# A two-layer transformer on one core: the order of the seven products, the spread of the w2 butterflies, and DMA-turned probabilities for two more units of the first attention

## Chip, core and metric

The kernel runs on one core of a Trainium2 chip. Its time is the device time of one execution in microseconds (us); the median of 3 runs of the kernel before is 749.98 us (749.78 to 750.11). The engines are TensorE (PE for matmuls, PEld for its weight loads), VectorE (DVE), ScalarE (ACT), GpSimd (POOL) and SyncE (SP), whose queue issues all DMAs here. An engine works its own queue strictly in order, and waits where an instruction's input, or the buffer that it writes, isn't ready.

## What is computed

Four layers, one after the other, on x of 4 sequences x 256 tokens x 256 features in fp32. Each adds its result to x and begins with a layer norm. Cut to its core, the reference is

```python
# layer 0, attention: 16 query heads, 8 key/value heads, window 128
q, k, v = einsum(x, q_kernel), einsum(x, k_kernel), einsum(x, v_kernel)
q, k = rope(rms_norm(q)), rope(rms_norm(k))
probs = softmax(where(mask, q @ k.T * 0.088, -big))
x = x + einsum(probs @ v, out_kernel)
# layer 0, FFN
h = silu(x @ w_gate) * (x @ w_up)
x = x + keep_two_largest_of_four(h) @ w_down
# layer 1, attention: 16 heads, causal
k, q, v = W_K x, W_Q x, W_V x
x = x + W_O (softmax(mask(k, q) / sqrt(128)) @ v)
# layer 1, FFN
hidden = fwht(silu(x @ W1.T) * (x @ W3.T))     # Walsh-Hadamard transform over 1024
x = x + hidden @ W2.T
```

## The kernel before, in words

**Layout.** A tile has 128 partitions. A sequence has two tiles of 128 tokens. Everything is fp32, and an fp32 matmul is two TensorE passes in the trace (x2 rows), while a transpose of a 128 x 128 tile is one. PSUM, where matmuls write, has eight banks; pool `ps1` (`bank()`) rotates four, and the other four belong by turns to `ps2` (`half()`, `wide()`) and `st_pool` (`st()`).

**Units and stages.** Each attention runs over 16 units of work, one for a sequence and a group of four heads. In the first attention unit n is sequence n // 4, group n % 4; in the second it is sequence n % 4, group n // 4. `pipelined` calls the stages of a unit in successive steps, so that several units are under way at once, and after each step calls what stands in `behind` for it (mostly output projections). In `attention0` the stages are project, rotate, turn, score, split, join and attend, with lags 0, 0, 1, 2, 3, 4, 4, called within a step in the order project, join, split, score, rotate, turn, attend. The calls set each instruction's place in the program; a scheduler then fixes the order within each engine's queue when the program is built, and `issue_after` pins an instruction behind another one of its engine.

**First attention.** `project0` multiplies (rows pj, L437), DVE forms the rope parts qs and qc (L442), `rotate0` adds them (L461), sums squares (ss, L462) and lets POOL make the factors r (L481) and scale k (L484). q is turned from the sixth unit on by a DMA (`qpl`, `qplT`), k by TensorE (tr_k, L510), which ACT copies (kT, L511). `probabilities` makes scores (sc, L204 and L205), masks them with a running maximum on DVE (L207), exponentiates on ACT with row sums (L217) and scales on POOL by the reciprocal (L225). Each unit has two pairs of heads, kk = 0 and 1, each with a tile p of 128 x 768.

**Turning the probabilities.** p @ v needs p with the tokens turned. There are two ways. By DMA: `planes` lets POOL separate p into 16-bit halves (pl, L242), a DMA transposes them (plT, L251), and `joined` puts the halves together again (pT, L262), in the first attention with one ACT copy for each pair. By TensorE: `transposed` makes six transposes of 128 x 128 for each pair (tr_p, L237), and ACT and DVE copy three each (pT, L238). In the first attention the DMA way serves all units but the last three (13, 14 and 15), in the second all but the last two. The tiles pl and plT of the first attention share four buffers. Then come av (L385, L389), its copy zT (L393) and the output projection po (L294).

**The seven products.** The second attention's q, k and v and the last FFN's two hidden products are formed by 2 x 2 blocks with seven block products in place of eight. `left_of` (L615) and `right_of` (L624) make the sums of blocks on DVE; `seven_products` issues the products into three PSUM accumulators x, z and y and combines them through copies u on ACT (L632, L638, L641, L650) and sums on DVE (L635, L644, L647). In `project1` the generators for q and k (banks qk_x, qk_z, qk_y) and for v (bank v_x, and one bank v_zy that holds z in its first half and y in its second) advance in turn. For each product the first flag says whether it begins a new accumulation in its bank.

**Butterflies.** The Walsh-Hadamard transform is folded into w2. `hadamard` does the part within 128 rows on TensorE (ph, L793) with an ACT copy (L796), and three rounds of sums and differences across row groups on POOL (L805), four instructions each. Before, `prepare` and its neighbours call one round behind each of the steps 11 to 14 of the second attention (the first call is the TensorE part).

Of the kernel before, what the change touches and what calls it, by code (L numbers as in the profile page):

```python
# [24 lines left out]
ALU = mybir.AluOpType  # L25
AX = mybir.AxisListType

P = 128
B, T, D = 4, 256, 256
# [19 lines left out]
def two_layers(ctx, tc, consts, tables, x, wq, wkv, wo, w_gate, w_up, w_down,  # L49
               w_k, w_q, w_v, w_o, w1, w3, w2, out):  # L50
    nc = tc.nc
# [92 lines left out]
    last_of = {}  # L144
# [94 lines left out]
        return pT  # L239

    def copy_gpsimd(o, i):
        nc.gpsimd.tensor_scalar(o, i, 1.0, 1.0, ALU.mult, ALU.mult)  # L242

    def planes(p, tile):

# [70 lines left out]
    def attention0():  # L316
        with tc.tile_pool(name="attn0", bufs=2, reuse_waits="tile", side="right") as own:
            xnT, factors = {0: normed(0)}, {}


            cos_s = own.tile([P, NT, 2, HD], F32, name="cos_s", bufs=1)
            sin_s = own.tile([P, NT, 2, HD], F32, name="sin_s", bufs=1)
            with tc.issue_after(last_of["norm"].ins):
                for t in range(NT):
                    for tab, at in ((cos_s, 0), (sin_s, 256)):
                        src = angles[:, at + t * HD : at + (t + 1) * HD]
                        nc.vector.tensor_tensor(
                            tab[:, t], src.unsqueeze(1).to_broadcast([P, 2, HD]), scl, ALU.mult
                        )

            def project(n, _):
                b, g = divmod(n, 4)
                held = project0(own, xnT[b], g, cos_s, sin_s)
                if g == 1 and b + 1 < B:
                    factors[b + 1] = moments(b + 1)
                if g == 2 and b + 1 < B:
                    with tc.issue_after(last_of["qc"].ins):
                        xnT[b + 1] = normed(b + 1, factors[b + 1])
                return held

            def rotate(n, held):
                rot, v = held
                rot, qT_planes, r = rotate0(rot, n >= 6, last_of["mx"] if 2 <= n < 14 else None)
                return rot, qT_planes, v, r

            def turn(n, held):
                rot, qT_planes, v, r = held
                return *turn0(own, rot, qT_planes, half if 6 <= n < 14 else bank), v, r

            def score(n, held):  # L350
                qT, kT, v, r = held
                ps = [
                    probabilities(
                        qT, kT, (2 * kk, 2 * kk + 1), mask0,
                        r[:, :, 2 * kk : 2 * kk + 2].rearrange("p t h -> p h t"),
                    )
                    for kk in range(2)
                ]
                return ps, v

            def split(n, held):
                ps, v = held
                return ps if n >= B * 4 - 3 else [
                    planes(p, own_planes) for p in ps
                ], v

            def own_planes(shape, name):
                return own.tile(shape, U16, tag="pl", name=name, bufs=4)

            def join(n, held):  # L370
                ps, v = held
                return [
                    transposed(ps[kk]) if n >= B * 4 - 3 else joined(ps[kk], ((
                        (nc.scalar.copy, slice(0, 2), last_of["exp"]),
                        (nc.scalar.copy, slice(0, 2), last_of["exp"]),
                    )[kk],)) for kk in range(2)
                ], v

            def attend(n, held):
                pTs, v = held  # L380
                zT = page("zT")
                for kk in range(2):
                    pT = pTs[kk]
                    av = bank([2, T], "av")
                    nc.tensor.matmul(  # L385
                        av, lhsT=v[:, 0, kk, :], rhs=pT[:, :, 0:T], start=True, stop=False,
                        skip_group_check=True,
                    )
                    nc.tensor.matmul(  # L389
                        av[:, :, P:T], lhsT=v[:, 1, kk, :], rhs=pT[:, :, T:],  # L390
                        start=False, stop=True, skip_group_check=True,
                    )
                    nc.scalar.copy(zT[:, 2 * kk : 2 * kk + 2, :], av)  # L393
                return zT

            def out(b, t, gs, kept=False):

                def emit(done):
                    zTs, w = [done[4 * b + g] for g in gs], wo_sb[:, 4 * gs[0] :]
                    if not kept:  # L400
                        project_out(bank([D], "po"), zTs, w, b, t)
                    else:
                        with tc.issue_after(last_of[0].ins):
                            project_out(half([D], "po"), zTs, w, b, t)
                return emit

            behind = {
                4 * b + 6 + 2 * k + t: [out(b, t, (2 * k, 2 * k + 1))]
                for b in range(B) for k in range(2) for t in range(NT)
            }  # L410
            behind = {step: fns for step, fns in behind.items() if step < 16}
            behind[17] = [lambda _: xn_f.append(normed(0))]
            behind[19] = [
                lambda _: xn_f.append(normed(1)), *(out(2, t, (2, 3), True) for t in range(NT)),
                *(out(3, t, (0, 1, 2, 3)) for t in range(NT)),
            ]
            pipelined(
                (project, rotate, turn, score, split, join, attend), (0, 0, 1, 2, 3, 4, 4),
                behind, (0, 5, 4, 3, 1, 2, 6),
            )  # L420
# [203 lines left out]
            nc.vector.tensor_tensor(t[i], a, b, op)  # L624
        return w11, w21, w22, t[3], t[0], t[1], t[2]

    def seven_products(product, x, z, y, c11, c12, c21, c22, shape):


        u = [late.tile(shape, F32, tag="u", name="u", bufs=4) for _ in range(3)]  # L630
        product(x, 1, True)
        nc.scalar.copy(u[0], x)  # L632
        yield
        product(z, 2, True)
        nc.vector.tensor_tensor(c11, z, u[0], ALU.add)  # L635
        yield
        product(y, 5, True)
        nc.scalar.copy(u[1], y)  # L638
        yield
        product(x, 6, False)  # L640
        nc.scalar.copy(u[2], x)  # L641
        yield
        product(y, 3, False)
        nc.vector.tensor_tensor(c12, y, u[2], ALU.add)  # L644
        yield
        product(x, 7, False)
        last_of["sum"] = nc.vector.tensor_tensor(c22, x, u[1], ALU.add)  # L647
        yield
        product(x, 4, False)
        last_of["copy"] = nc.scalar.copy(c21, x)  # L650
        yield
# [23 lines left out]
    def attention1(finish_ffn0):  # L675
# [48 lines left out]
        behind = {n + 3: [out(n)] for n in range(9)}  # L724
        behind[0] = [lambda _: finish_ffn0()]

        def prepare(_):
            w2h.extend(hadamard(w2_raw))
            w2h[1][0](_)

        behind.setdefault(11, []).append(prepare)
        for i in range(1, 4):
            behind.setdefault(11 + i, []).append(lambda _, i=i: w2h[1][i](_))

        def prepare_ffn1(_):
            with tc.issue_after(last_of["sum"].ins):
                r_ffn1.extend(factors_ffn1(half) for half in range(2))

        behind[15] = [out(12)]
        behind[16] = [  # L740
            lambda _: xn_f.append(normed(0)),
            prepare_ffn1,
        ]
# [8 lines left out]
    def project1(x, w):  # L752
# [11 lines left out]
        def product_v(o, i, first):  # L764
# [10 lines left out]
        zy = st([P, 2, 256], "v_zy")  # L775
        products.append(seven_products(
            product_v, bank([256], "v_x"), zy[:, 0], zy[:, 1],
            *(c[:, t, m, :] for t in range(2) for m in range(2)), [P, 256],
        ))
        for _ in zip(*products):  # L780
            pass
# [3 lines left out]
    def hadamard(w2_raw):  # L785


        a, b = (late.tile([P, NF, D], F32, tag=t, name=f"w2_{t}") for t in ("qkw", "qkt"))

        def within(_):  # L790
            for f in range(0, NF, 2):
                ph = bank([2, D], "ph")
                nc.tensor.matmul(  # L793
                    ph, lhsT=had, rhs=w2_raw[:, f : f + 2, :], start=True, stop=True
                )
                nc.scalar.copy(a[:, f : f + 2, :], ph)  # L796

        def across(s, src, dst):
            i = src.rearrange("p (a two s) d -> p a two (s d)", two=2, s=s)
            o = dst.rearrange("p (a two s) d -> p a two (s d)", two=2, s=s)  # L800
            half = s * D // 2
            for k, op in enumerate((ALU.add, ALU.subtract)):
                for n in range(2):
                    cols = slice(n * half, (n + 1) * half)
                    nc.gpsimd.tensor_tensor(  # L805
                        o[:, :, k, cols], i[:, :, 0, cols], i[:, :, 1, cols], op
                    )

        return b, (
            within, lambda _: across(1, a, b), lambda _: across(2, b, a),  # L810
            lambda _: across(4, a, b),
        )

    def factors_ffn1(half):

# [150 lines left out]
```

## Time and profile before

| what | value |
|---|---|
| median of 3 runs | 749.98 us |
| the profiled execution's own time | 749.92 us |
| its span, first to last instruction | 748.1 us |
| PE busy | 737.5 us, 99% of the span |
| ACT / DVE / POOL busy | 401.6 / 465.9 / 331.0 us |
| granted TensorE clock | 1.00 in every slice |
| end of the first attention (last av) | about 264.5 us after the span's start |
| second attention | about 357 to 665 us |
| last FFN | about 665 us to the end |

The execution's own time is 1.8 us more than the span: what lies before the first and behind the last profiled instruction. A row of the timeline reads: start, length, engine, line, operation, output <- inputs, count, and in brackets the idle time of the engine ahead of it with what ended it. Matmuls overlap, so the length of a row of matmuls says less than the distance between starts: in this trace one pass with a moving tile of 128 columns starts 0.111 us after the one before, one with 256 columns 0.216 us, one with 512 columns 0.43 us, wherever nothing is waited for.

### The profile page before, as it was taken

The numbers are of one execution on the slowest core, as the hardware profiler recorded it, in microseconds if no ns is written. First come the engines' busy times: TensorE is split into PE (matmuls) and PEld (weight loads), VectorE is DVE, ScalarE is ACT, GpSimd is POOL, SyncE is SP. The second block draws the span as 40 slices with busy tenths as digits, with TensorE's granted clock in tenths as the row PEclk, the third lists the DMA queues.
The fourth block names the chain that finished last, engine by engine and source line by source line (L and its number), as shares of the span: only waits on it lengthen the run. The fifth ranks groups of instructions, "written<-read, shape, count | busy, mean of one in ns | idle before, by whom it ended". The sixth has DMA issues, their size and how long they took to land.

```text
span 748.1 us, 11666 instructions
## 1 busy us (share of the span) xinstructions
PE 737.5 (99%) x3980; PEld 603.2 (81%) x3980; DVE 465.9 (62%) x1402; ACT 401.6 (54%) x985; POOL 331.0 (44%) x475
## 2 busy tenths in 40 slices
PE   8999999999999999999999999999999999999998
PEld 5556566666666788888899999999998899899997
DVE  6999877888877418976655644464443448354433
ACT  2487887667778712322355555555554675314332
POOL 1587978887899401011135433343338554210000
PEclk9999999999999999999999999999999999999999
DMA  8733255434454060002235322523232222001100
GB/s 326 285 64 57 50 99 88 74 69 90 76 96 74 1 225 15 15 15 74 68 71 108 105 43 43 135 64 43 44 71 43 43 43 42 2 0 23 28 8 28
DMA packets 121610, 53.30 MB, mean 71 GB/s; under 512 B 114768, under 2 KB 116944, under 8 KB 120784
## 3 DMA queue, kind: packets, MB, share of 16 engines
q1 hardware_dynamic: 121552, 52.57, 30.4%
q8 instruction: 31, 0.51, 0.3%
q14 instruction: 27, 0.22, 0.1%
HBM read 22.94 MB, written 1.05 MB: 32 GB/s over the span
## 4 chain that ended last, share of the span: by engine, by line
PE 42%; POOL 3%; DVE 2%; ACT 2%; DMA 1%; issue 1%; POOLq 0%
PE po L282 6%; PE qk_x L759 6%; PE gu_x L829 4%; PE po_f L587 4%; PE av L270 3%; PE qk_y L759 3%; PE sc L205 3%; PE v_x L765 3%; PE v_zy L765 2%; PE gu_y L829 2%; PE av L273 2%; PE sc L204 1%; POOL w_qkt L805 1%; PE qk_z L759 1%; ACT p L217 1%; PE gu_z L829 1%
## 5 line engine op out<-in xcount | busy, mean ns | idle before, releaser
L225 POOL TENSOR_SCALAR p<-p,rs 128x128 f32<-128x128 f32 (+1 forms) x256 | 116.8, 474 | 157.7 <-DVE rs L222 154.2
L207 DVE CUSTOM_DVE_ANT_0 p<-sc,cst 128x128 f32<-128x128 f32 (+1 forms) x256 | 79.4, 352 | 10.5 <-PE sc L205 8.3
L242 POOL TENSOR_SCALAR pl<-p 128x1536 uint16<-128x1536 uint16 x54 | 79.5, 1473 | 3.5
L217 ACT ACTIVATE p<-p,nb,r 128x128 f32<-128x128 f32 (+1 forms) x128 | 68.3, 535 | 19.9 <-DVE nb L214 19.8
L262 ACT COPY pT<-plT 128x768 uint16<-128x768 uint16 (+1 forms) x54 | 76.6, 1478 | 1.7 <-DMA plT<-pl 1.7
L437 PE MATMUL pj<-wq,xnT 128*128 128x512 f32 x128 | 61.1, 596 | 1.8 <-DVE qT L500 1.1
L437 PE MATMUL pj<-wkv,xnT 128*128 128x512 f32 x128 | 60.3, 592 | 0.0
L217 ACT ACTIVATE p<-p,nb 128x128 f32<-128x128 f32 (+1 forms) x128 | 56.3, 444 | 7.1 <-DVE nb L212 7.1
L294 PE MATMUL po<-wo,zT 128*128 128x256 f32 x256 | 57.9, 379 | 0.0
L282 PE MATMUL po<-w_o,zT 128*128 128x256 f32 x256 | 57.7, 379 | 0.0
L155 POOL TENSOR_SCALAR ve<-mv 128x2 f32<-128x2 f32 x16 | 3.5, 220 | 118.4 <-DVE mv L152 118.0
L447 ACT ACTIVATE sq<-pj 128x512 f32<-128x512 f32 x64 | 31.0, 490 | 44.3 <-DVE qc L442 43.8
L294 PEld LDWEIGHTS po<-wo,zT 128*128 128x128 f32 x256 | 48.2, 190 | 6.9 <-ACT kT L511 0.6
L282 PEld LDWEIGHTS po<-w_o,zT 128*128 128x128 f32 x256 | 47.5, 190 | 5.8
L437 PEld LDWEIGHTS pj<-wkv,xnT 128*128 128x128 f32 x128 | 24.3, 190 | 30.2 <-issue 28.2
L437 PEld LDWEIGHTS pj<-wq,xnT 128*128 128x128 f32 x128 | 23.6, 190 | 25.4 <-issue 20.2
L442 DVE TENSOR_TENSOR qs<-pj,sin_s 128x512 f32<-128x512 f32 x64 | 35.3, 552 | 13.9 <-PE pj L437 13.5
L270 PE MATMUL av<-pT,v 128*128 128x256 f32 x128 | 38.9, 385 | 1.3 <-DVE mx L207 1.1
L650 ACT COPY qk<-qk_x 128x512 f32<-128x512 f32 x16 | 9.4, 586 | 53.9 <-PE qk_x L759 53.9
L644 DVE TENSOR_TENSOR qk<-qk_y,u 128x512 f32<-128x512 f32 x16 | 11.1, 692 | 43.6 <-PE qk_y L759 42.5
L205 PE MATMUL sc<-qk 128*128 128x256 f32 x128 | 38.2, 380 | 0.0
L205 PE MATMUL sc<-kT,qT 128*128 128x256 f32 x128 | 38.2, 380 | 0.0
(154 smaller groups left out, 1787.4 us busy)
## 6 DMA issues: line engine op xcount, KB each, us to landing
w<-in_w_dram SPq DMA_DIRECT2D x3, 1024.0 KB, 4.9
wq<-in_wq_dram SPq DMA_DIRECT2D x4, 512.0 KB, 8.0
wkv<-in_wkv_dram SPq DMA_DIRECT2D x4, 512.0 KB, 7.9
wo<-in_wo_dram SPq DMA_DIRECT2D x4, 512.0 KB, 10.2
w_qk<-in_w_q_dram SPq DMA_DIRECT2D x4, 512.0 KB, 4.9
w_qk<-in_w_k_dram SPq DMA_DIRECT2D x4, 512.0 KB, 6.0
w_v<-in_w_v_dram SPq DMA_DIRECT2D x4, 512.0 KB, 7.0
w_o<-in_w_o_dram SPq DMA_DIRECT2D x4, 512.0 KB, 6.4
```

Of the source, the lines that this page charges most:

```text
L205: nc.tensor.matmul(sc[:, P : 3 * P], lhsT=q[:, P:T], rhs=k, start=True, stop=True)
L207: last_of["mx"] = nc.vector.tensor_tensor_reduce(out=p[:, j, cols], in0=sc[:, cols], in1=mask[:, cols], scale=1.0, scalar=-3.0e38, op0=ALU ...
L217: last_of["exp"] = nc.scalar.activation(p[:, j, cols], p[:, j, cols], AF.Exp, bias=nb[:, j, i : i + 1], scale=SCALE1 if rq is None else rq ...
L225: nc.gpsimd.tensor_scalar(p[:, j, cols], p[:, j, cols], rs[:, j, i : i + 1], 1.0, ALU.mult, ALU.mult)
L242: nc.gpsimd.tensor_scalar(o, i, 1.0, 1.0, ALU.mult, ALU.mult)
L262: copy(words.rearrange("p (n w) -> p w n", w=2), halves[:, :, js].rearrange("p w j n -> p w (j n)"),)
L270: nc.tensor.matmul(av, lhsT=v0, rhs=pT[:, 0:T], start=True, stop=False, skip_group_check=True)
L282: nc.tensor.matmul(po[:, t, :], lhsT=zT[:, j, t * P : (t + 1) * P], rhs=w[:, j, :], start=(t == j == 0), stop=(j == 3), skip_group_check=True,
L294: nc.tensor.matmul(po, lhsT=zTs[hd // 4][:, hd % 4, t * P : (t + 1) * P], rhs=w[:, hd, :], start=(hd == 0), stop=(hd == n - 1),)
L437: last_of[0] = nc.tensor.matmul(pj, lhsT=xnT[:, c, cols], rhs=w[:, g, c, :], start=(c == 0), stop=(c == NC - 1),)
L759: last_of[1] = nc.tensor.matmul(o[:, j, :], lhsT=wqk[i - 1][:, j // 2, j % 2, :], rhs=x[i - 1], start=(first and j == 0), stop=True, skip_ ...
L829: nc.tensor.matmul(o[:, j, :], lhsT=r[j // 2][i - 1][:, j % 2, :], rhs=x[i - 1], start=(first and j == 0), stop=True, skip_group_check=True,)
```

## The change

Four edits. (1) In `seven_products` the fifth product, into y, comes first, then the first (into x), the second (into z) and the others as before; for v, where y and z share a bank, the fifth now opens the bank and the second no longer does (`z_alone=False`). (2) In the first attention units 13 and 14 are turned by DMA too, so only unit 15 goes over TensorE. (3) For units 14 and 15 `rotate0` is called inside project, ahead of the other units' score in the same step. (4) The twelve butterflies are separate pieces, four behind each of the steps 11 to 13, and each is pinned behind the latest POOL copy that `copy_gpsimd` recorded.

```diff
--- before.py
+++ after.py
@@ -239,7 +239,7 @@
         return pT
 
     def copy_gpsimd(o, i):
-        nc.gpsimd.tensor_scalar(o, i, 1.0, 1.0, ALU.mult, ALU.mult)
+        last_of["planes"] = nc.gpsimd.tensor_scalar(o, i, 1.0, 1.0, ALU.mult, ALU.mult)
 
     def planes(p, tile):
 
@@ -336,12 +336,15 @@
                 if g == 2 and b + 1 < B:
                     with tc.issue_after(last_of["qc"].ins):
                         xnT[b + 1] = normed(b + 1, factors[b + 1])
-                return held
-
-            def rotate(n, held):
+                return held if n < 14 else rotated(n, held)
+
+            def rotated(n, held):
                 rot, v = held
                 rot, qT_planes, r = rotate0(rot, n >= 6, last_of["mx"] if 2 <= n < 14 else None)
                 return rot, qT_planes, v, r
+
+            def rotate(n, held):
+                return rotated(n, held) if n < 14 else held
 
             def turn(n, held):
                 rot, qT_planes, v, r = held
@@ -360,7 +363,7 @@
 
             def split(n, held):
                 ps, v = held
-                return ps if n >= B * 4 - 3 else [
+                return ps if n >= B * 4 - 1 else [
                     planes(p, own_planes) for p in ps
                 ], v
 
@@ -370,7 +373,7 @@
             def join(n, held):
                 ps, v = held
                 return [
-                    transposed(ps[kk]) if n >= B * 4 - 3 else joined(ps[kk], ((
+                    transposed(ps[kk]) if n >= B * 4 - 1 else joined(ps[kk], ((
                         (nc.scalar.copy, slice(0, 2), last_of["exp"]),
                         (nc.scalar.copy, slice(0, 2), last_of["exp"]),
                     )[kk],)) for kk in range(2)
@@ -624,18 +627,18 @@
             nc.vector.tensor_tensor(t[i], a, b, op)
         return w11, w21, w22, t[3], t[0], t[1], t[2]
 
-    def seven_products(product, x, z, y, c11, c12, c21, c22, shape):
+    def seven_products(product, x, z, y, c11, c12, c21, c22, shape, z_alone=True):
 
 
         u = [late.tile(shape, F32, tag="u", name="u", bufs=4) for _ in range(3)]
+        product(y, 5, True)
+        nc.scalar.copy(u[1], y)
+        yield
         product(x, 1, True)
         nc.scalar.copy(u[0], x)
         yield
-        product(z, 2, True)
+        product(z, 2, z_alone)
         nc.vector.tensor_tensor(c11, z, u[0], ALU.add)
-        yield
-        product(y, 5, True)
-        nc.scalar.copy(u[1], y)
         yield
         product(x, 6, False)
         nc.scalar.copy(u[2], x)
@@ -726,18 +729,20 @@
 
         def prepare(_):
             w2h.extend(hadamard(w2_raw))
-            w2h[1][0](_)
+            w2h[1](_)
 
         behind.setdefault(11, []).append(prepare)
-        for i in range(1, 4):
-            behind.setdefault(11 + i, []).append(lambda _, i=i: w2h[1][i](_))
+        for i in range(12):
+            behind.setdefault(11 + i // 4, []).append(
+                lambda _, i=i: w2h[2][i](last_of["planes"].ins)
+            )
 
         def prepare_ffn1(_):
             with tc.issue_after(last_of["sum"].ins):
                 r_ffn1.extend(factors_ffn1(half) for half in range(2))
 
-        behind[15] = [out(12)]
-        behind[16] = [
+        behind.setdefault(15, []).append(out(12))
+        behind[16] = behind.get(16, []) + [
             lambda _: xn_f.append(normed(0)),
             prepare_ffn1,
         ]
@@ -775,7 +780,7 @@
         zy = st([P, 2, 256], "v_zy")
         products.append(seven_products(
             product_v, bank([256], "v_x"), zy[:, 0], zy[:, 1],
-            *(c[:, t, m, :] for t in range(2) for m in range(2)), [P, 256],
+            *(c[:, t, m, :] for t in range(2) for m in range(2)), [P, 256], z_alone=False,
         ))
         for _ in zip(*products):
             pass
@@ -799,17 +804,21 @@
             i = src.rearrange("p (a two s) d -> p a two (s d)", two=2, s=s)
             o = dst.rearrange("p (a two s) d -> p a two (s d)", two=2, s=s)
             half = s * D // 2
-            for k, op in enumerate((ALU.add, ALU.subtract)):
-                for n in range(2):
-                    cols = slice(n * half, (n + 1) * half)
-                    nc.gpsimd.tensor_tensor(
-                        o[:, :, k, cols], i[:, :, 0, cols], i[:, :, 1, cols], op
-                    )
-
-        return b, (
-            within, lambda _: across(1, a, b), lambda _: across(2, b, a),
-            lambda _: across(4, a, b),
-        )
+
+            def part(k, op, cols):
+                def emit(first):
+                    with tc.issue_after(first):
+                        nc.gpsimd.tensor_tensor(
+                            o[:, :, k, cols], i[:, :, 0, cols], i[:, :, 1, cols], op
+                        )
+                return emit
+
+            return [
+                part(k, op, slice(n * half, (n + 1) * half))
+                for k, op in enumerate((ALU.add, ALU.subtract)) for n in range(2)
+            ]
+
+        return b, within, across(1, a, b) + across(2, b, a) + across(4, a, b)
 
     def factors_ffn1(half):
 
```

In the program as built the three rounds of butterflies stand on POOL as three blocks of four: the first where it stood, the second behind the p and pl instructions of the next unit, the third behind those of the unit after. PE's queue holds 24 transposes fewer, POOL's four copies pl more, SP's four DMA transposes more, and ACT's two copies pT of 128 x 1536 halves for each of units 13 and 14 in the place of two of 128 x 384 words from PSUM.

## Prediction

> **What bounds the kernel now.** I read the busy line first, then a table of stretches, then the timeline of the places where the diff acts, engine by engine.
>
> ```profile
> PE 737.5 (99%) x3980; PEld 603.2 (81%) x3980; DVE 465.9 (62%) x1402; ACT 401.6 (54%) x985; POOL 331.0 (44%) x475
> ```
>
> TensorE is the bound: the other engines matter only where TensorE waits for them. I took the starts of all its matmuls and subtracted the pitch of each (0.111, 0.216, 0.43 us by width): the excess is 19.4 us in the whole span, 4.1 of it in the first 20 us. So a gain has two sources: passes that vanish, and the few stalls among those 19.4 us. The stalls near the edits:
>
> ```profile
> 254.45 1.46 PE L294 MATMUL po<-wo,zT 128*128 128x256 f32 x6
> 256.20 0.52 PE L237 MATMUL tr_p<-cst,p 128*128 128x128 f32 x3 [0.29 <-ACT zT L393]
> ```
> ```profile
> 476.91 1.05 PE L759 MATMUL qk_y<-xs,t_qk 128*128 128x128 f32 x8
> 477.83 0.70 PE L765 MATMUL v_zy<-t_v,xs 128*128 128x256 f32 x2
> 478.36 1.05 PE L759 MATMUL qk_x<-xs,t_qk 128*128 128x128 f32 x8
> ```
> ```profile
> 595.90 0.38 PE L273 MATMUL av<-pT,v 128*128 128x128 f32 x2
> 597.37 0.67 PE L270 MATMUL av<-pT,v 128*128 128x256 f32 x2 [1.09 <-DVE mx L207]
> ```
>
> The reader is to see, in the first, starts that don't meet (six passes from 254.45 fill 1.30 us, the next starts at 256.20: 0.45 lost). In the second, two passes lasting to the next start take 0.53 where 0.43 is their pitch: 0.10 lost, and so in 14 of 16 units; with two longer ones (377.80, 0.59; 602.30, 0.45) the stalls around v_zy are 2.75 us. In the third, 1.25 us (597.37 less 595.90 + 0.22). The releaser named there had long been done; the DMA behind pT landed at 596.1 and ACT's copy followed.
>
> **A, end of the first attention (units 13, 14 turned by DMA).** It removes 24 transposes: 24 x 0.111 = -2.66. The stalls among them between 240 and 262 (0.45, 0.23, 0.09, 0.03) go: -0.80. What comes instead:
>
> ```profile
> L237 PE MATMUL tr_p<-cst,p 128*128 128x128 f32 x60 | 8.3, 274 | 0.3 <-ACT zT L393 0.3
> L242 POOL TENSOR_SCALAR pl<-p 128x1536 uint16<-128x1536 uint16 x54 | 79.5, 1473 | 3.5
> L262 ACT COPY pT<-plT 128x1536 uint16<-128x1536 uint16 x26 | 48.6, 1926 | 0.0
> ```
>
> Four pl copies on POOL are 5.9 us; it was busy 10.65 of 20 us in 240 to 260 and once idle for 5.4, so they fit. SP's four transposes stand ahead of the second attention's weight loads; those start at 264.80 and are read from 282.62, so a few us are free. A transpose of this kind landed 3.6 to 4.0 us after its issue: unit 14's halves would land at about 255 and 257. DVE loses four tr_p copies (0.56 each). ACT trades four copies of 0.48 for four of 1.85: +5.5 us, in a stretch where it is already the second-busiest:
>
> ```profile
> 240.00:260.00 20.00, 19.71 (x100) 14.81 (x99) 11.39 (x51) 15.94 (x46) 10.65 (x23) 1.00 0.00 1
> ```
> ```profile
> 251.24 0.49 ACT L217 ACTIVATE p<-p,nb,r 128x128 f32<-128x128 f32 x1 [2.52 <-DVE nb L214]
> ```
>
> Columns of the table: stretch, length, then busy time of PE, PEld, DVE, ACT, POOL. ACT has 4.06 us free in 20, 2.52 of them in one wait. Besides, moving the sums of units 14 and 15 ahead puts a DVE sum (0.95) and reduction (0.94) in front of unit 12's and 13's maxima, so nb(13), at 232.29 before, comes 1.9 later, and the exponentials of unit 13 start at 234.4, not 233.06. From there ACT's queue is a chain with no wait left: exps(13) 4.2, kT 0.3, zT 0.95, pT(12) 3.7, exps(14) 4.25, kT 0.5, zT 0.95, pT(13) 3.7, exps(15) 4.25, zT 0.95, xnT 0.5, pT(14) 3.7 = 27.95, to 262.35. TensorE, never waiting, would go from av(11) at 234.55 through what stands ahead of the second half of av(14): av(11) 2.57, po 3.45, sc(14) 2.62, tr_k 0.44, av(12) 2.57, po 1.73, sc(15) 2.62, av(13) 2.57, tr_n 0.44, po 3.45, pgu 0.86, half of av(14) 1.29, po 0.43 = 25.04 (each is its count of passes by the pitch), to 259.6. So it waits there about 2.75 us, in one or several pieces. The eight po and four gate matmuls that the scheduler put around av(14) and av(15) are in that sum; they fill, and vanish from where they stood.
>
> A = -2.66 - 0.80 + 2.75 = **-0.7**. Ends: -3.5, if ACT's chain has slack that I don't see; +0.8, if the nb on its path are held up. Those two prices are in the trace: an nb is 0.16, but 0.84 at 216.33 and 0.99 at 218.86, both beside a running POOL copy, and two or so would lie in the chain. I take the chain as timed.
>
> The Trainium skill, "SBUF — State Buffer", section "Who interferes with whom", says that GpSimd shares a port pair with VectorE and that one holds it for a whole instruction; it speaks against the change, which puts 5.9 us more of GpSimd beside short VectorE steps. The two slow nb rows agree with it; by it alone A would be near +0.8, the end given above.
>
> **B, product order (16 units of the second attention).** Before, the y half of v_zy waited for DVE's sum out of the z half of the same bank:
>
> ```profile
> 477.36 0.41 DVE L635 TENSOR_TENSOR v<-v_zy,u 128x256 f32<-128x256 f32 x1
> ```
>
> It ends at 477.77, and TensorE starts at 477.83; two blocks on, it waits again a little. After, y comes first. Counted from the group's start by the pitches (0.89 for eight passes of qk, 0.43 for two of v): y5 for v ends at 1.32, ACT's copies of y (0.59, 0.38) are done at about 2.05, and z2 for v starts at 3.53: 1.5 us spare. x6 for qk (3.96) needs ACT's copies of x1, done at 3.0 to 3.4. y3 for v (6.17) needs DVE's sum out of z, done at about 4.8. DVE has had 1.5 us idle ahead of that sum. No wait is left inside a unit: B = **-2.75**. Ends: -2.75 (nothing else is there to gain) and 0 (a new wait of the old length).
>
> **C, butterflies.** Before, three rounds stood together on POOL:
>
> ```profile
> 579.42 5.18 POOL L805 TENSOR_TENSOR w_qkt<-w_qkw 128x512 f32<-128x512 f32 x4
> 584.56 1.65 POOL L225 TENSOR_SCALAR p<-p,rs 128x128 f32<-128x128 f32 x4
> ```
>
> The factors rs for that p were ready at 583.05 (its row starts at 582.87 and lasts 0.18), so the p started 1.5 us late, and its pl, DMA, pT and the av at 597.37 with it. Now only the first round stands before these p; the p start with rs, 1.5 us sooner, and the 1.25 stall goes. The other two rounds (5.3 us each) stand behind later units' pl, where POOL was idle 8.8 us (before 599.72) and 7.7 us (before 613.75): hidden, and if a round overran its gap, the next p and its av would be that much later. C = **-1.25**. Ends: -1.25, as no other stall hangs on these p, and 0. DVE's pT copies took 1.31 (576.93) and 1.12 (578.69) beside butterflies, 0.59 elsewhere; that now falls on other units' copies; no stall stood behind those two, and two such delays of 0.6 before an av would be the 0 end.
>
> **D, last FFN (8 halves).** Same order. The y3 passes that waited for ACT's copy of y5 lose 0.39 in all. x6 now follows x1 by two groups instead of three, and the first half's start changes: I take 8 x 0.05 + 0.2 against it. D = **+0.2**, from -0.4 to +0.9.
>
> **Sum.** -0.7 - 2.75 - 1.25 + 0.2 = -4.5. The profiled execution took 749.92 (span 748.1 and 1.8 around it), which is the median of the runs within 0.06: 749.9 - 4.5 = **745.4 us**. Its own range, from half of the distances to the ends, is 743.9 to 746.9.
>
> **Rivals.**
> R1, ScalarE keeps up: no stall in A (its waits for nb, 2.52 at 251.24, show that it has had slack). 745.4 - 2.75 = 742.7.
> R2, the products gain nothing: z2 for v shares a bank with y5 and now waits for ACT's copy. If that ends over 3.5 us into the group, 1.5 later than computed, the old 0.17 per unit returns: 745.4 + 2.75 = 748.1. It would take ACT standing in exponentials at the group's start. Against it: in the unit shown ACT waited 2.29 us for qk_x before its first copy at 475.41. The Trainium skill, "PSUM — Partial Sum Buffer", section "PSUM bank collisions raise a hardware error", asks for semaphores by bank, not by address; the 477.77 and 477.83 above agree, and by it z2 must wait for ACT although it writes the other half.
> R3, A at its dear end: nb held up beside POOL's added copies, 745.4 + 1.5 = 746.9, and 748.4 if unit 15's chain loses the same again. For it: the two rows of nb; against it: the six rows of nb from 232.29 on take 0.14 to 0.17.
> R4, slower: y3 for v waits for DVE's sum out of z, with 6.17 - 4.8 = 1.37 us spare. DVE works in order, and if the maxima of another unit's scores (0.352 each) come ahead of that sum, more than four of them use the margin up. Six would cost 6 x 0.352 - 1.37 = 0.74 in each of 16 units, 12 in all: 757. It is slower from a wait of 0.37 a unit on, which is five of them. Against it: DVE was idle for 1.53 us right ahead of that sum (476.75), and no maxima lie in 474 to 481.
>
> **How the numbers follow.** Chances: forecast 0.55, R1 0.13, R2 0.15, R3 0.09, R4 0.08. 0.2%, 1.5 us, is about what a measurement of this kernel can tell from no change. Forecast and R1 are faster by more (0.68); of R2 about half is (0.07) and of R3 half (0.05): faster 0.80, same 0.11, slower 0.09. The range goes from R1, 742.5, to the upper ends of R2 and R3, 748.5; outside are R4 and the tails of R1 and R2.
>
> **What would show it.** A: 36 rows tr_p, not 60; stalls before av(13) or av(14) with ACT busy without a break from 234 to 262; if ACT idles there, A is wrong. B: two v_zy passes 0.43 apart from the next block, in all units. C: no gap near 597, and p directly after its rs near 583. D: y3 with no wait, x6 with little. A wait of TensorE for ACT in each unit's products, or av waits beyond 600 behind late p, would make the prediction wrong.

## The result and the profile after

The changed kernel takes **746.64 us** (median of 6 runs, 746.36 to 747.09) against 749.93 for the kernel before, run beside it: ratio 0.9957, 95% interval 0.9945 to 0.9970. Measured a second time, the same file gave 747.57 (746.76 to 748.60) against 750.14: 0.9968 (0.9956 to 0.9979). The forecast was 745.4, range 742.5 to 748.5. It was right in sign and range, and the gain is 2.6 to 3.3 us, not 4.5.

The page's busy line, then the table of stretches (columns as in the prediction):

```profile
PE 734.0 (99%) x3956; PEld 599.4 (80%) x3956; DVE 464.3 (62%) x1398; ACT 405.8 (54%) x985; POOL 338.2 (45%) x479
```
```profile
240.00:260.00 20.00, 19.21 (x88) 14.10 (x87) 10.59 (x51) 20.00 (x45) 16.91 (x30) 1.00 0.44 79
```

TensorE has its 24 passes fewer and is still busy 99%. In 240 to 260, ACT went from 15.94 to 20.00 of 20 us: it never pauses, and TensorE, which had 0.29 us free there, now has 0.79.

To place the rest, I cut each profiled execution at two marks, the first product of the second attention and the first product of the last FFN, and summed in each part by how much every matmul starts later than its pitch allows ("excess"). The last part is counted to the start of the last matmul.

| profiled execution | start to 2nd attention | 2nd attention | last FFN |
|---|---|---|---|
| before | 357.37 | 307.28 | 79.87 |
| after | 356.74 | 304.00 | 80.32 |
| after, run again | 358.18 | 304.00 | 80.32 |

The second and third columns repeat within 0.02 us from one execution to the next; the first doesn't, which is a subject of its own below. Against the recorded terms: by the first column A is -0.6 in one execution and +0.8 in the other (forecast -0.7); B and C together -3.28 (forecast -4.0); D +0.45 (forecast +0.2).

**A.** TensorE's and ACT's timelines of the changed kernel:

```profile
253.24 1.12 PE L388 MATMUL av<-pT,v 128*128 128x512 f32 x2 [0.27 <-ACT pT L262]
...
258.89 1.13 PE L545 MATMUL pgu<-xnT,w_gate 128*128 128x256 f32 x4 [0.20 <-ACT xnT L179]
260.70 1.12 PE L388 MATMUL av<-pT,v 128*128 128x512 f32 x2 [0.68 <-ACT pT L262]
```
```profile
249.42 3.77 ACT L262 COPY pT<-plT 128x1536 uint16<-128x1536 uint16 x2
...
258.73 3.68 ACT L262 COPY pT<-plT 128x1536 uint16<-128x1536 uint16 x2
```

Each new wait of TensorE ends with an ACT instruction. The stalls between 243 and 263 add up to 2.8 us (forecast 2.75), and ACT's last pT copy of unit 14 ends at 258.73 + 3.68 = 262.4 (forecast 262.35).

**B.** The products of one unit, where the first and the second v_zy now lie three blocks apart:

```profile
473.27 1.05 PE L764 MATMUL qk_y<-xs,t_qk 128*128 128x128 f32 x8
474.17 0.60 PE L770 MATMUL v_zy<-t_v,xs 128*128 128x256 f32 x2
474.60 1.05 PE L764 MATMUL qk_x<-xnT,w_qk 128*128 128x128 f32 x8
...
476.81 0.60 PE L770 MATMUL v_zy<-w_v,xnT 128*128 128x256 f32 x2
477.25 1.05 PE L764 MATMUL qk_x<-xs,t_qk 128*128 128x128 f32 x8
```

Two passes of v_zy fill 0.43 to the next start, with nothing lost. The excess around v_zy fell from 2.95 to 0.13 us. But 0.9 came back in the first units: the excess ahead of av at 399 to 402 grew from 0.45 to 1.16, and that ahead of x4 at 366 from 0.38 to 0.60.

**C.** The p of POOL and the av that had stalled:

```profile
580.99 1.64 POOL L225 TENSOR_SCALAR p<-p,rs 128x128 f32<-128x128 f32 x4 [8.62 <-DVE rs L222]
582.71 1.47 POOL L242 TENSOR_SCALAR pl<-p 128x1536 uint16<-128x1536 uint16 x1
```
```profile
594.04 0.39 PE L273 MATMUL av<-pT,v 128*128 128x128 f32 x2
594.27 0.60 PE L270 MATMUL av<-pT,v 128*128 128x256 f32 x2
```

p starts as soon as its rs is there (580.71 + 0.18), and the av follow each other at their pitch: the 1.25 us and the 0.07 after it are gone.

### The profile page after: what moved, and what is told of

Its sections match the earlier page's. It is cut to its first block, busy times and chain, and to the rows that moved or that the text cites. A ratio compares the mean times of both kernels' runs of the same rounds, so it can differ in the third digit from the quotient of the medians.

```text
span 744.8 us, 11648 instructions
## 1 busy us (share of the span) xinstructions
PE 734.0 (99%) x3956; PEld 599.4 (80%) x3956; DVE 464.3 (62%) x1398; ACT 405.8 (54%) x985; POOL 338.2 (45%) x479
## 4 chain that ended last, share of the span: by engine, by line
PE 87%; DVE 8%; ACT 3%; POOL 1%; issue 1%; ACTq 0%; DVEq 0%; POOLq 0%
PE pj L440 11%; PE po L282 7%; PE pgu L545 7%; PE qk_x L764 7%; PE po_f L590 7%; PE po L294 6%; PE sc L205 6%; PE gu_x L838 4%; PE av L270 4%; PE qk_y L764 3%; PE v_x L770 3%; PE av L388 3%; PE sc L204 3%; PE v_zy L770 3%; PE gu_y L838 2%; PE av L273 2%
## 5 line engine op out<-in xcount | busy, mean ns | idle before, releaser
L242 POOL TENSOR_SCALAR pl<-p 128x1536 uint16<-128x1536 uint16 x58 | 87.8, 1513 | 4.0
L262 ACT COPY pT<-plT 128x1536 uint16<-128x1536 uint16 (+1 forms) x58 | 84.0, 1509 | 0.0
L217 ACT ACTIVATE p<-p,nb,r 128x128 f32<-128x128 f32 (+1 forms) x128 | 68.2, 534 | 18.7 <-DVE nb L214 18.6
L484 POOL TENSOR_TENSOR r<-ve,mhalf 128x12 f32<-128x12 f32 x16 | 37.3, 2328 | 0.8
```

The costliest lines, as they stand in the source:

```text
L217: last_of["exp"] = nc.scalar.activation(p[:, j, cols], p[:, j, cols], AF.Exp, bias=nb[:, j, i : i + 1], scale=SCALE1 if rq is None else rq ...
L242: last_of["planes"] = nc.gpsimd.tensor_scalar(o, i, 1.0, 1.0, ALU.mult, ALU.mult)
L262: copy(words.rearrange("p (n w) -> p w n", w=2), halves[:, :, js].rearrange("p w j n -> p w (j n)"),)
```

## The experiments

Theory, after this comparison: the four edits act in three stretches by the mechanisms of the prediction, and what is missing came back in the first units of the second attention and in the last FFN. Rival: the gain belongs to something that the edits move without meaning to. The runs found both.

### Each edit alone

**Product order alone** (the diff's edit 1).

> Only the order of the seven products is changed, from the kernel before. Theory (the changed kernel's trace): the v_zy waits of 2.9 us go, but 0.9 comes back in the first units, where the av that wait for their softmax are reached sooner, and the last FFN pays 0.45: about -1.6 us, 748.3. Rival 1, the recorded term: the products alone give -2.75 + 0.2 = -2.55, 747.4, and what came back belongs to another edit. Rival 2: they give nothing by themselves, 749.9, since the stall at 597 takes it.

748.67 us (11 runs), ratio 0.9982 (0.9974 to 0.9991); second attention 305.69, last FFN 80.32. In the trace the stalls around v_zy are gone (2.95 to 0.13), the av near 400 and the last FFN pay what they pay in the changed kernel, and the stall at 597 has grown by 0.37, because TensorE gets there sooner. The theory holds in what goes and what comes back, and falls short by those 0.37, which it left out; both rivals fall.

**Butterflies alone** (edit 4).

> Only the butterflies are spread, from the kernel before. Theory: the 1.25 us stall at 597 goes and its restart, 0.1, with it: -1.35 us, 748.6, with the two rounds hidden in POOL's idle time. Rival: the slower copies on VectorE beside them take it back: 749.9 or more.

747.71 us (6 runs), ratio 0.9970 (0.9959 to 0.9981); second attention 305.47: -1.81, of which 1.32 is the stall at 597 and 0.4 the wait of v_zy at 602. The theory holds, and in the second attention the edit gives a little more than it said. The rest isn't its work: the profiled execution began the second attention at 356.42, 0.95 sooner than before, and nothing that the edit touches runs ahead of that.

**First attention alone, with and without the earlier sums** (edits 2 and 3; edit 2).

> Only units 13 and 14 by DMA and the sums of 14 and 15 sooner, from the kernel before. Theory: 24 transposes (-2.66) and the old stalls (-0.8) go, ScalarE's chain costs 2.8: -0.6 us, 749.3, with ScalarE busy without a break from about 234 to 262. Rival: the stalls in the changed kernel came from the other edits, none of which works before 357 us: then -3.4, 746.5.

> As the run before, but with the sums of units 14 and 15 where they stood. Theory A: the sums ahead of the maxima cost 1.5 us at the head of ScalarE's chain (exponentials of unit 13 from 234.6, not 233.1), so that without the move the stalls shrink by about that: -2.0 us, 747.9. Theory B: unit 14's scores hang on those sums through POOL's r and the turned k, so that without the move the exponentials of unit 14 come later than ScalarE could start them, by 1 us or more: 0 to +1 us, 750 to 751.

With the sums sooner 748.89 (ratio 0.9987, 0.9978 to 0.9996), without 750.09 (1.0003, 0.9994 to 1.0012). The wait of theory B is there, as TensorE's timeline without the move shows:

```profile
241.43 0.60 PE L205 MATMUL sc<-kT,qT 128*128 128x256 f32 x2
245.18 1.01 PE L510 MATMUL tr_k<-cst,qc 128*128 128x128 f32 x4 [3.16 <-POOL qc L484]
```

POOL's new pl copy stands ahead of the qc that tr_k turns, and TensorE waits 3.3 us. But its price isn't what the medians say. In the profiles the second attention begins at 358.06 without the move and at 357.93 with it: the move takes this wait away, and other waits come in its place. The difference of the medians goes with the clock. Without the move, nine of the eleven runs show a granted clock of 0.995 to 0.998, lower than any run of another kernel here, and take 749.46 to 751.39; the two at 1.000, the profiled one among them, take 748.82 and 749.09, against 748.69 to 749.07 with the move. Whether the wait of 3.3 us is what lowers the clock isn't shown.

And the first of these two kernels is not fast for the reason expected. Its second attention begins at 357.93, **later** than before (357.37). Its gain is in the second attention, 305.83 for 307.28, which the edit doesn't touch: the stall at 597 is gone there too, and in the other kernel as well (305.85), with the butterflies where they always stood.

### Why the stall at 597 goes without a butterfly moved

VectorE's rs, POOL's p and pl lie as before in that kernel, counted from the second attention's start; the DMA differs. Before, the pl ended at 590.94 and the last piece of its transpose landed at 596.1, 5.1 us later; here it took 3.75. The DMA view of the transfer before (592 to 595.5; by queue: packets, MB, share; last, issue to landing) has a packet of another queue:

```profile
q1 hardware_dynamic: 1568, 0.39, 63.9%
q8 instruction: 1, 0.02, 1.6%
plT<-pl SPq DMA_TRANSPOSE x1, 5.1
```

That packet, 16 KB at 593.71, is an instruction fetch. In the packet lists there is one for every 128 TensorE passes or so (31 in 3980 passes); that they belong to TensorE is inferred from that count. I took all transfers plT of the second attention in the fourteen traces that no other transfer follows within 6 us: in all but four of the some 120 without such a fetch in that time the last piece starts 3.2 to 3.6 us behind pl (in the four, whose fetch begins 3.3 to 3.4 behind, 4.3); in the 26 with a fetch that begins 0.9 to 3.1 us behind pl, 3.9 to 4.7. The 24 passes fewer move every later fetch by 24/128 of its period of about 18.6 us, some 3.5 us by this reckoning, and the transfer is missed; in the kernel with edits 2 and 3 that fetch lies 3.2 us later than before, counted from the second attention's start. To test it, the kernel before gets 24 passes more, which moves the fetches the other way, and nothing else:

```diff
-    for i in range(12):
+    for i in range(24):
         nc.tensor.matmul(
-            idle[:, i % 4, :], lhsT=zeroes[:, 0:P], rhs=zeroes[:, P:], start=True, stop=True
+            idle[:, i % 4, 0:64], lhsT=zeroes[:, 0:P], rhs=zeroes[:, P : P + 64],
+            start=True, stop=True,
         )
```

> From the kernel before: the 12 matmuls on zeroes at the start are 24 of half the width, so that their time stays and TensorE has 24 passes more in its program. In the traces one 16 KB instruction fetch comes for every 128 passes, and a transfer plT that such a fetch meets lands 1.3 us later (last packet 4.5 us behind pl, not 3.2). Theory: the stall of 1.25 us near 597 needs both the late p and the fetch that met that transfer at 593.7; the fetch moves 3.5 us forward, to about 590, misses it, and the stall goes: -1.3, 748.5, with no butterfly moved. Rival: the butterflies alone made the stall and it stays: 749.9.

755.80 us, ratio 1.0081 (1.0067 to 1.0094): as a whole slower, since passes of half the width start no sooner than the others and the first projection begins at 13.54 us, not 8.28. From there on the expectation holds: the fetch lies 2.6 us sooner, counted in the same way. The same DMA view of this kernel, and its av:

```profile
q1 hardware_dynamic: 1571, 0.39, 61.9%
plT<-pl SPq DMA_TRANSPOSE x1, 3.6
```
```profile
603.38 0.38 PE L274 MATMUL av<-pT,v 128*128 128x128 f32 x2
603.61 0.60 PE L271 MATMUL av<-pT,v 128*128 128x256 f32 x2
```

No fetch in the transfer, landing after 3.6 us, no stall; the second attention takes 305.80, 1.48 less than before. So the stall had two causes, and it needed both: p 1.5 us late behind the butterflies, and a fetch that made the transfer 1.35 us longer. Taking away the fetch is enough, as three kernels with the late p show. That taking away the late p is enough by itself is argued from the sizes and not shown: with the butterflies alone spread, pl ended 1.9 us sooner, counted from the second attention's start, and its transfer had landed 3.7 us behind pl when the fetch began, so both causes went at once. In the changed kernel both are gone too, and the gain is had once: that is the larger part of why the gains of the single edits (1.15, 2.11 and 0.93, in all 4.2) are more than the whole.

### The first attention: more than one outcome of one program

**The changed kernel again, and without its first-attention edits** (edits 1 and 4 only).

> The changed kernel once more. In its first profile the first attention ended 0.6 us sooner than before (second attention's first product at 356.74); in three builds with the same program up to there it came 1.5 us later (357.9 to 358.2), with one VectorE sum at 215 us at 1.91 us, not 1.32. Theory: it is one program with two outcomes, and which one comes is settled by which of VectorE and GpSimd is there first; single runs then lie at about 746.6 or about 748.1. Rival: the changed kernel is always the quick one, 746.4 to 747.1 in all runs.

> The changed kernel without its edits to the first attention (units 13 to 15 by TensorE, sums where they stood): product order and butterflies alone. Theory: those edits are worth next to nothing (-0.6 in the one profile, +0.9 in the others), so this is as fast as the changed kernel within 0.6 us: 746.3 to 747.2; the stall at 597 stays away, since the p are early. Rival: they carry the -0.7 that was forecast, or more by moving TensorE's instruction fetches: 747.4 or more.

747.57 against 747.13 (746.68 to 747.53; ratio 0.9959, 0.9945 to 0.9973) on the same chip. The six runs of the changed kernel fall in two groups, 746.76, 747.04, 747.05 and 748.09, 748.14, 748.60. The theories hold: without the first attention's edits the kernel is as fast, second attention and last FFN being the same to 0.01 us (304.01 and 80.32). Only one of the six is profiled, 748.09 of the slower group, so what separates the groups is read from two profiles, near 215 us. VectorE and POOL in the first profile of the changed kernel (TensorE's second attention from 356.74):

```profile
215.06 1.32 DVE L464 TENSOR_TENSOR qc<-qc,qs 128x768 f32<-128x768 f32 x1
216.30 0.94 DVE L465 TENSOR_REDUCE ss<-sq 128x6 f32<-128x768 f32 x1
...
218.27 0.15 DVE L214 SCALAR_TENSOR_TENSOR nb<-mx,r 128x4 f32<-128x4 f32 x1
```
```profile
215.53 2.18 POOL L242 TENSOR_SCALAR pl<-p 128x1536 uint16<-128x1536 uint16 x1
```

and in the second (from 358.18):

```profile
215.31 1.91 DVE L464 TENSOR_TENSOR qc<-qc,qs 128x768 f32<-128x768 f32 x1
217.15 0.94 DVE L465 TENSOR_REDUCE ss<-sq 128x6 f32<-128x768 f32 x1
...
219.12 0.99 DVE L214 SCALAR_TENSOR_TENSOR nb<-mx,r 128x4 f32<-128x4 f32 x1
```
```profile
214.95 1.47 POOL L242 TENSOR_SCALAR pl<-p 128x1536 uint16<-128x1536 uint16 x1
```

This sum is one that edit 3 moved: in the kernel before it stands behind that nb, at 217.99. In the first, VectorE's sum is under way when POOL comes, and POOL's copy takes 2.18 for 1.47 (the sum takes 1.32 itself, for 0.95 alone: it began beside POOL's scaling of k, 214.38 to 215.57). POOL comes later there because its factors r, at 211.2, took 3.09 us, not 2.28; what made them differ isn't followed further back. In the second, POOL is first, VectorE's sum (0.95 alone) takes 1.91 and ends 0.8 behind POOL's copy, and the nb behind it meets the next POOL copy (qpl, from 218.05) and takes 0.99 for 0.15. Then the exponentials, ACT's chain and TensorE are late. The Trainium skill, "SBUF — State Buffer", section "Who interferes with whom", says that the issue order decides which of the two engines waits, and that a reduction on VectorE doesn't contend at all; both agree with these rows (the reduction takes 0.94 in each). Here the two engines arrive 0.47 and 0.36 us apart, in opposite order, and one program has two times.

What these edits are worth is read best from the stretch where they act. From 200 to 265 us the excess is 0.87 to 0.96 us in the six profiles without them. With them it is 3.0 in the first profile of the changed kernel and 4.2 in four others (the second one, the two edits alone, and the kernels of the next section with one mend each). Less the 2.66 of the vanished passes, that is a gain of 0.5 or a loss of 0.7. The rest of the first column's spread lies ahead of 200 us, where these edits change nothing: without the kernel with more passes at its start, the excess there lies between 8.1 and 9.4 us.

**Two pT copies to VectorE** (`last_of["rs"]` is the last reciprocal of L222, recorded there; the choice for `n == 14` is never taken). The edit's main part:

```diff
-                        (nc.scalar.copy, slice(0, 2), last_of["exp"]),
-                        (nc.scalar.copy, slice(0, 2), last_of["exp"]),
-                    )[kk],)) for kk in range(2)
+                        (nc.vector.tensor_copy, slice(0, 2), last_of["nb" if n == 14 else "rs"])
+                        if (n, kk) in ((12, 1), (13, 0)) else
+                        (nc.scalar.copy, slice(0, 2), last_of["exp"])
+                    ),)) for kk in range(2)
```

> From the changed kernel: of the first attention's last copies pT, one of unit 12 and one of unit 13 go to VectorE (3.7 us off ScalarE's chain). Theory: ScalarE's chain bounds the end of the first attention, but behind it stand the maxima, which can't be ready before 243.4 and 251.7, so that only 0.9 of the 2.8 us of stalls goes: 745.7. Rival 1: ScalarE alone bounds it: -2.4, 744.2. Rival 2: the copies hold up VectorE's reciprocals or collide with GpSimd, and nothing is won: 746.6 or more.

746.71 (746.00 to 748.27; ratio 0.9960, 0.9948 to 0.9973). The profiled execution has the late start (0.67 lost at 217) and yet begins the second attention at 356.71, 1.5 sooner than the changed kernel with that start (its stalls from 243 to 263 are 2.2 us there, not 3.3); but the spread of the runs is as large as the gain. ACT then waits for maxima, as the theory said:

```profile
244.24 0.49 ACT L217 ACTIVATE p<-p,nb,r 128x128 f32<-128x128 f32 x1 [1.68 <-DVE nb L214]
```

So in this execution ScalarE's chain bounds the stretch, and 3.7 us off it took 1.2 us of the stalls, 0.9 by the theory. Whether the median gains is left open by five runs, and one more profile of the same first attention, below, came out the other way.

### What came back

**Old order in the last FFN alone.**

```diff
-        product(y, 5, True)
-        nc.scalar.copy(u[1], y)
-        yield
+        def fifth():
+            product(y, 5, True)
+            nc.scalar.copy(u[1], y)
+
+        if y_first:
+            fifth()
+            yield
...
+        if not y_first:
+            fifth()
+            yield
         product(x, 6, False)
...
-            *(c[:, :, m, t, :] for t in range(2) for m in range(2)), [P, 4, P],
+            *(c[:, :, m, t, :] for t in range(2) for m in range(2)), [P, 4, P], y_first=False,
```

> From the changed kernel: the last FFN alone has the old product order again. Theory: its waits go back from 2.72 to 2.27 us: -0.45, 746.2. Rival: the order is worth nothing there and the 0.45 came from what precedes it: 746.6.

747.35 us (ratio 0.9966, 0.9954 to 0.9979), by the whole time not to be told from the changed kernel; the first attention came out late (358.21). The last FFN alone is plain: 80.32 goes back to 79.86, and the theory holds.

**The fourth sum of blocks later.** Here VectorE's timeline of the changed kernel shows a sum of 128 x 128 that takes 1.43 us beside POOL's pl (397.02 to 398.49) where its neighbours take 0.26 to 0.48, and the nb behind it; the av at 402.43 wait for a pT copy that ACT can begin only after the exponentials of that nb:

```profile
396.59 0.48 DVE L618 TENSOR_TENSOR xs<-xs,xnT 128x128 f32<-128x128 f32 x1
397.20 1.43 DVE L618 TENSOR_TENSOR xs<-xnT,xs 128x128 f32<-128x128 f32 x1
399.38 0.15 DVE L212 TENSOR_SCALAR nb<-mx 128x4 f32<-128x4 f32 x1
```
```profile
402.43 0.70 PE L270 MATMUL av<-pT,v 128*128 128x256 f32 x2 [0.68 <-ACT pT L262]
```

In the kernel before, the same sum took 0.32 us, beside POOL's p; with the products' new order POOL's p and its pl come some 3 us sooner (p at 395.15), and the pl falls on the sum. The kernel with the product order alone shows the 1.43 us too. VectorE and POOL before:

```profile
398.34 0.32 DVE L615 TENSOR_TENSOR xs<-xnT,xs 128x128 f32<-128x128 f32 x1
```
```profile
398.33 2.38 POOL L225 TENSOR_SCALAR p<-p,rs 128x128 f32<-128x128 f32 x4 [2.98 <-DVE rs L222]
```

```diff
-            nc.vector.tensor_tensor(s[:, i], a, b, op)
+            if i == 3 and later is not None:
+                later.append(lambda _, s=s, x12=x12: nc.vector.tensor_tensor(
+                    s[:, 3], x12, s[:, 1], ALU.subtract))
+            else:
+                nc.vector.tensor_tensor(s[:, i], a, b, op)
...
-                    left[b + 1] = left_of(xn1[b + 1])
+                    left[b + 1] = left_of(xn1[b + 1], behind[2] if b == 2 else None)
```

> From the changed kernel: the fourth sum of blocks xs for the fourth sequence, which took 1.43 us beside a GpSimd copy pl (0.29 elsewhere), is computed later, behind the maxima. Theory: that sum held up the maxima, nb, the exponentials and the av near 402: the 0.85 us wait there shrinks to 0.15 to 0.3, 746.0. Rival: the next VectorE step, a copy pT, is held up by the same GpSimd copy and the wait stays: 746.6.

747.26 us (ratio 0.9965, 0.9952 to 0.9977), again with a late first attention (358.14). The second attention goes from 304.00 to 303.45, its excess ahead of the av at 402 from 0.85 to 0.28: the theory holds. In that kernel the next VectorE copy meets the POOL copy instead (1.40 us for 0.59), as its rival said; the nb behind it is still 0.56 sooner, counted from the second attention's start. So most of the 0.7 that came back ahead of the av is this meeting of sum and copy.

**All three mends, and the mends without the first attention's edits.**

> The changed kernel with the three edits that took a wait away: one pT copy of unit 12 and one of 13 on VectorE (-1.5 against builds of the same state), old product order in the last FFN (-0.45), fourth sum of blocks later (-0.55). Theory: they are in three different stretches and add up: 2.5 below the slow outcome of the changed kernel, 1 to 2 below its median: 745.2. Rival: a wait removed early is paid at the next softmax, and it stays at 746.

> Product order in the second attention alone, butterflies spread, fourth sum of blocks later, and the first attention as in the kernel before. Theory: from the second attention's start the time is that of the kernel with the three mends (3.8 us less than before), the first attention neither gains nor loses and has only the small spread of the kernel before (0.5): 749.9 - 3.8 = 746.1. Rival: the first attention's edits were needed so that the second starts well, and this stays at 747.1, as without the mends.

All three on the changed kernel: 747.58 (ratio 0.9965, 0.9953 to 0.9978). The second attention and the last FFN take 303.47 and 79.87, the two mends there adding up to 1.0, but the first attention came out at 358.76, and all five runs are near it. The theory's sum fails in the first attention and there alone. That stretch is the same program as in the kernel with the two pT copies on VectorE, and here the copies win nothing: the stalls from 243 to 264 add up to 4.3 us. ScalarE waits 2.41 us for an nb that takes 1.13 beside POOL's pl (243.70), and 1.74 us for a transpose. What made POOL's order come out otherwise isn't shown. The last kernel leaves that stretch as it was: **746.04** (745.68 to 746.67; ratio 0.9947, 0.9933 to 0.9961), as forecast, with 303.47 and 79.88: the lowest median of all, with the product order in the second attention alone, the butterflies spread and the fourth sum later. That it beats the kernel before is sure; the interval of its ratio overlaps that of the changed kernel, and the surer ground there is the 1.0 us less behind the first attention.

## Why the prediction was right, and where it was not

- **A, -0.7: the mechanism was right in one outcome, and the gain isn't shown.** In the first profile ScalarE's chain runs without a break (27.00 of 27 us busy from 235 to 262) and ends within 0.1 us of the forecast, and the stalls are 2.8 for 2.75. But nb beside POOL, entered as the dear end of the range (+0.8), is another outcome: in the edits' own stretch -0.5 or +0.7. That the first measurement met the forecast here was luck. In the seven profiles with edits 2 and 3 the second attention begins between 356.7 and 358.8, 357.8 in the mean; in five without them between 356.4 and 357.7, 357.3 in the mean (the kernel with more passes at its start left out). R3, given 0.09, describes three of the six runs of the second measurement, and four of the five profiles that have the changed kernel's first attention or the two edits alone.
- **B, -2.75: mis-sized.** The v_zy stalls went as worked out (2.8), and no unit got a new wait inside its products, so R2 and R4 fall. The step that failed is "no wait is left inside a unit", taken for the whole edit: ahead of the units' av 0.7 came back, and 0.2 ahead of x4. TensorE gets to the av near 402 some 0.7 us sooner and its pT isn't ready any sooner, since VectorE's slowed sum holds up the nb; the prediction followed TensorE's waits inside a unit, and not what the new order moves on VectorE and POOL. In the second attention the order alone gives -1.6 with the 597 stall grown, and in the whole change -2.0.
- **C, -1.25: right in size (1.32), with half of its cause unseen.** The prediction took the landing after 5.1 us as given; it noted 3.6 to 4.0 elsewhere and didn't ask why this one was longer. An instruction fetch lay in it. That the earlier p alone would have saved the 1.25 isn't shown.
- **D, +0.2: +0.45, mis-sized.** x6 and x7 each lose 0.05 us or more in every half, where 0.05 for x6 and 0.2 for the first half's start were entered: together they lose 0.98 more than before. y3 gets back 0.53, where 0.39 was entered.
- **The sum, -4.5:** -3.45 by the three columns of the two profiled executions, which is A -0.6, B -2.0, C -1.3 and D +0.45; -3.3 between these executions as a whole and between the medians, -2.6 in the second measurement. R1 (ScalarE keeps up) fell by ACT's 20.00 of 20.

## What to carry to other kernels

When an edit removes a wait, follow TensorE to the next place where it depends on a chain that the edit didn't make sooner, and look at what the edit moves on the engines of that chain; the gain is paid back there first. Before putting a stall down to one late instruction, compare the durations along its chain with their usual values: here one transfer was 1.4 us longer than its kind, and without that the late instruction cost nothing. Compare stretches between marks in two traces before the whole times; a stretch that repeats within 0.02 us tells an edit of 0.5 us that medians can't.

## What the runs showed of the hardware

- A 16 KB instruction fetch comes for about every 128 TensorE passes and takes 0.9 to 1.4 us on one DMA queue; the last piece of a transpose of 128 x 1536 halves that it meets starts 3.9 to 4.7 us behind its source, not 3.2 to 3.6. Taking 24 passes away near 250 us moved the fetch near 594 us by 3.2 us, and 24 added at the start moved it the other way by 2.6; both took a stall of 1.3 us away there.
- A wait of TensorE ahead of 256-column passes costs about 0.1 us more, also a short one: in 21 of 22 places of the kernel before, the pass behind the one that waited starts 0.29 to 0.32 after it, not 0.216 (477.83 there; 399.05, 402.43 and 634.98 after). Not every wait does: behind that of 0.45 us at 256.20, ahead of transposes, it is 0.03. Eleven of the v_zy stalls were nothing but that, behind a wait of about 0.02.
- VectorE copies of 128 x 1536 halves took 1.0 us where ScalarE takes 1.85 to 1.93.
